# A window-attention and linear-attention kernel: layer 0's means subtracted on VectorE, its factors spread by kind, the last softmax inverse formed in SBUF, and another order

## The chip, the cores and the metric

The kernel runs on one core of one Trainium2 chip. The metric is the device time of one execution in microseconds (us). PE is TensorE, DVE is VectorE, ACT is ScalarE, POOL is GpSimd and SP is SyncE; ACT's and SP's queues also issue the DMAs of this kernel.

## The reference, cut to what matters

The input has 4 images of 128 channels and 64 x 64 pixels. Layer 0 norms over channels, adds a 3 x 3 depthwise convolution, and attends inside windows of 16 x 16 pixels, each query over its 5 x 5 neighbours. The patches are padded with zeros, so a neighbour outside the window counts with a logit of 0: it adds exp(0) = 1 to the denominator. Layer 1 is causal linear attention over the 4096 pixels of an image, then a recurrence over them with a batch norm in front.

```
# layer 0
y = _layernorm2d(x, ln_g, ln_b)                      # over channels
y = y + _cpe(y, cpe_w, cpe_b)                        # 3 x 3, depthwise
q, k, v = einsum(windows of y, Wq / Wk / Wv)         # 2 branches, 4 heads of 32
k_nb, v_nb = _patches(k, 5), _patches(v, 5)          # zero padded at the window's edge
attn = softmax(einsum(q, k_nb) * scale, axis=neighbours)
yb = (ho[:, 0] + LAM * ho[:, 1:].sum(axis=1)) / rect # ho: einsum(attn, v_nb), then Wo
x = x + yb
# layer 1
t = t + _L1_attn_ref(_ln_t(t), W, b)                 # elu + 1 features, causal sums
t = t + _L1_ffn_ref(_ln_t(t), W, V, gamma, beta)     # y_t = sigmoid(w_t + y_{t-1} V^T)
```

## The kernel before

**Tiling.** The work is cut into 16 bands (4 images, 4 bands of 16 rows each) and 64 windows, four a band; `places[i]` is the band and the column of window i. Layer 1 takes a band in two halves, called `a` and `c`; the halves of the band before it are `y` and `z` there. Where the order of the tail needs older ones, they are `v` and `w`.

**Layer 0's norm.** For bands 2 to 15 `norm_rows(n)` norms in two groups of tokens, of 4 columns of 128 tokens in the first and 3, 4 or 5 in the second. `measure_rows(g)` takes mean and variance on DVE from a copy of x with tokens on partitions, and POOL packs the means and forms the inverse deviations into `pk`. SP stores `pk` in DRAM (`sent`, a row of 2k numbers for each token), and `spread_rows(g)` on ACT's queue loads it back into every partition, as the tile `ahead`. There is one buffer for `ahead` and one for `rows`, so the spread and the load of the second group wait for the scaling of the first. `centre(g)` subtracts the means from `rows` on POOL (L413), `scale(g, ...)` multiplies by `ln_g` and the inverse deviation on DVE into the padded image `ypad` (L424). Both read the factors with a step of 2k elements. POOL then copies the edges of `ypad`, and the depthwise convolution runs as nine taps, the first on ACT (L498), the others on DVE (L500).

**Windows.** `window_inputs` makes q, k and v; `logits` the exponentials `es`; `weighted` has three steps. `sums` adds up the exponentials on PE and ACT copies them to `den` (L647), from which a DMA of SP collects one copy into `dc`. `values` forms the weighted values, which ACT copies to `o_sb` (L667). `inverse` adds the count of padded neighbours `pad_c` (L670) and takes the reciprocal (L672) on DVE, stores it in DRAM (`rd`, L676) and loads it spread over partitions (`rden`, L678); with every fourth window it checks the range of the sums (L633, L634). `scaled` multiplies `o_sb` by `rden` on POOL into the band's `oT` (L687).

**Layer 1.** `output0` projects `oT` on PE (L713) and adds x on DVE (L720). Then come `measure` and `norm` (POOL forms the inverse deviation, L314 and L315), `turn`, the features `queries` and `keys`, `values`, `scores`, `accumulate` (the running states, L822), `attend0` and `attend1` (L833 and L835 on PE; L843, L844 and L847 on DVE), `measure_last`, `send` (SP stores factors, L744), `spread` (ACT's queue loads them spread, L755), `keep` (L852) and `product` (L874, L875).

**Order.** PE, DVE, ACT and POOL run in the order in which the program is written: `in_order` ties each instruction to the one before it on its engine. SP is not tied. The order itself is in five tables. `START` has the first four windows. In the main loop each window goes through `SLOT`, in which names are steps of windows i-2 to i+1 and numbers are six gaps. In a gap the generator `layer1` advances by one entry of `LAYER1` (24 entries, over four windows, beginning with gap 0 of a band's second window), and then `front` by as many steps as `AHEAD[wj]` names that gap. `front` goes through `FRONT`: `n` is a step of the next band's norm, `d` and `c` pieces of the two halves of the convolution. `TAIL` has what is left after the last window's logits. After the first five entries of `FRONT`, which `START` does, the first number of `AHEAD` belongs to its sixth entry. `warm.k` puts k matmuls of zeros on PE ahead of the next bank that is taken (L288). All PSUM work of layers 0 and 1 goes through one ring of eight banks.

After layer 1 a fixed loop of 41 rounds runs the recurrence. The change doesn't touch it.

Of the kernel before, what the change touches and what calls it, by code (L numbers as in the profile page):

```python
# [45 lines left out]
    "measure_last.z product.y output.a send.z",  # L46
    "",
    "",
    "measure.a",
# [4 lines left out]
    "turn.a spread.z",  # L54
    "keep.z",
    "queries.a",
    "values.a keys.a product.z turn.c",
    "",
    "scores.a turn_keys.a keys.c queries.c accumulate.a",
    "attend0.a",  # L60
    "attend1.a turn_keys.c",
    "",
    "measure_last.a values.c",
    "",
    "keep.a",
    "",
    "send.a spread.a scores.c accumulate.c",
# [3 lines left out]
SLOT = ("sums", "values", "scaled", "logits", 0, "inverse", 1, "q", 2, 3, "k", "v", 4, 5)  # L71
AHEAD = ("013344", "023345", "022345", "01123")
START = (
    "upper conv.1 lower q.0 k.0 front mul.2 v.0",
    "logits.0 front front q.1 k.1 front v.1 conv.3",
    "logits.1 sums.0 mul.2 values.0 inverse.0 front q.2 warm.3",
    "front scaled.0 front front k.2 front front v.2",
    "front front logits.2 sums.1 front prepare values.1 inverse.1",
    "front load.2 front q.3 k.3 v.3 front front",
    "front sums.2 warm.2 front q.4 values.2 inverse.2 k.4",  # L80
    "front scaled.1 v.4 warm.1 front logits.3",
)
TAIL = (
    "output.y inverse.62 warm.1 output.z scaled.61 measure.z norm.z turn.z",
    "values.z warm.2 sums.63 measure.y norm.y turn.y queries.y keys.y",
    "warm.1 values.63 keep.w turn_keys.y send.w scores.y keys.z inverse.63",
    "warm.4 scaled.62 values.y accumulate.y turn_keys.z spread.w scaled.63 attend0.y",
    "queries.z attend1.y warm.1 measure_last.y send.y spread.y scores.z accumulate.z",
    "output.a product.w keep.y measure.a attend0.z warm.2 output.c attend1.z",
    "norm.a warm.2 measure_last.z product.v measure.c norm.c product.y keep.z",  # L90
    "turn.a keys.a values.a turn.c queries.a keys.c queries.c warm.2",
    "turn_keys.a scores.a accumulate.a send.z attend0.a attend1.a measure_last.a send.a",
    "turn_keys.c warm.2 values.c scores.c accumulate.c attend0.c attend1.c spread.z",
    "spread.a measure_last.c warm.2 warm.4 keep.a norm_last.c product.z turn_last.c",
    "keep.c product.a product.c",
)
FIRST = "nnnnnncccccccccc"
FRONT = "ndnnddndnddnncccccccccc"
# [19 lines left out]
def conv_attn_hybrid(ctx: ExitStack, tc: tile.TileContext, ins: dict, out: bass.AP):  # L118
# [50 lines left out]
    def groups(n):  # L169
        wi = bands[n][1]  # L170
        first, end = (0 if wi == 0 else 1), NCH + (wi < NB - 1)
        return first, first + 4, end
# [202 lines left out]
    def norm_rows(n):  # L375
# [8 lines left out]
        def measure_rows(g):  # L384
# [15 lines left out]
            sent[g] = dram4.tile([P, 2 * k], F32, tag=f"ahead{k}", name=f"ahead{k}")  # L400
            nc.sync.dma_start(sent[g], pk[:, : 2 * k])

        def spread_rows(g):
            k = sent[g].shape[1]
            f = p1.tile([P, P * 2 * 5], F32, tag="ahead", name="ahead")
            f = f[:, : P * k].rearrange("p (t k) -> p t k", k=k)
            nc.scalar.dma_start(f, sent[g].unsqueeze(0).to_broadcast([P, P, k]))
            fac[g] = f.rearrange("p t (m j) -> p m j t", m=2)

        def centre(g):  # L410
            j0, j1 = groups(n)[g : g + 2]
            v = rows[n, g][:, : (j1 - j0) * P].rearrange("p (j t) -> p j t", t=P)
            nc.gpsimd.tensor_tensor(v, v, fac[g][:, 0], ALU.subtract)  # L413

        def scale(g, dst, t0, t1):
            x, r = rows[n, g], fac[g][:, 1, t0 // P : -(-t1 // P), :]
            if t1 - t0 < P:
                src = x[:, t0:t1].rearrange("p (r w) -> p r w", w=W)
                r = r[:, 0, : t1 - t0].rearrange("p (r w) -> p r w", w=W)
            else:  # L420
                src = x[:, t0:t1].rearrange("p (j a w) -> p j a w", a=2, w=W)
                r = r.rearrange("p j (a w) -> p j a w", w=W)
                dst = dst.rearrange("p (j a) w -> p j a w", a=2)
            nc.vector.scalar_tensor_tensor(dst, src, ln_g, r, ALU.mult, ALU.mult)  # L424
# [213 lines left out]
    def weighted(w):  # L638
# [29 lines left out]
        yield  # L668

# [298 lines left out]
    def block(what):  # L968
# [10 lines left out]
        elif name == "logits":  # L979
            logits(windows[i])  # L980
        elif name == "scaled":
            if i not in scales:
                scales.add(i)
                scaled(*places[i], windows.pop(i))
        elif name in ("sums", "values", "inverse"):
            if name == "sums" and ("weighted", i) not in steps:
                steps["weighted", i] = weighted(windows[i]), ["sums", "values", "inverse"]
            run_of, left = steps["weighted", i]
            if name in left:
                assert left.pop(0) == name  # L990
                next(run_of)
# [51 lines left out]
    which.update(a=Half(len(bands) - 1, 0), c=Half(len(bands) - 1, 1))  # L1043
    v0 = bank()[:, :1]
# [861 lines left out]
```

## Time and profile before

| | us |
|---|---|
| runs | 842.4, 845.6, 853.11 (median 845.6) |
| profiled execution, its own time | 848.08 |
| its span, first to last instruction | 846.4 |
| DVE taps of the convolution (L500) | 187.6 busy, 240 instructions of 128x512 |
| POOL products with the inverse (L687) | 83.6 busy, 64 instructions |
| POOL subtractions of the means (L413) | 42.5 busy, 28 instructions |
| DVE scalings (L424) | 34.6 busy (with the instructions of the same tile, counted without overlap), 48 instructions |
| chain of waits, by engine | PE 44%, DVE 38%, DMA 7%, issue 4%, POOL 3%, ACT 3% |

The span has five stages: the start with the first windows (to about 54 us), bands of 46 us in the main loop, the tail after the last window's logits (from 735), and the recurrence (from 792). "Busy" counts the time in which an engine has an instruction of that group; an idle time is put down to what ended it. A busy PE is not a PE at its peak, since the ends of matmuls are modelled. The mean TensorE clock granted was 0.988 of full.

### The profile page before, as it was taken

How to read it: one execution, taken by the hardware profiler on the slowest of the kernel's cores; microseconds unless marked ns; L12 is line 12 of the kernel's file. 1: busy time of each engine (PE TensorE's matmuls, PEld its weight loads, DVE VectorE, ACT ScalarE, POOL GpSimd, SP SyncE). 2: the span in 40 equal slices, each digit the busy share in tenths (PEclk: the TensorE clock that was granted, in tenths of full speed). 3: DMA queues.
4: the chain of work that ended last, by engine and by line, in shares of the span. 5: the costliest groups of instructions: out<-in, count | busy, mean ns of one | idle time of the engine just before them, and what ended most of it. 6: DMA issues, size and time to landing. Idle time of an engine off the chain costs nothing.

```text
span 846.4 us, 28848 instructions
## 1 busy us (share of the span) xinstructions
PE 800.7 (95%) x11719; PEld 634.6 (75%) x11719; DVE 714.6 (84%) x2075; ACT 503.9 (60%) x983; POOL 309.6 (37%) x413
## 2 busy tenths in 40 slices
PE   9979999999999999999999999999999998988893
PEld 6658878778777778787777877787877777766793
DVE  7657898998998999999999989989898985477884
ACT  4746667465757475665647575656667574613683
POOL 3033444334343333444343434334443312222094
PEclk9998999999999999999999999999999999999997
DMA  5123342443443433434344334333342322211797
GB/s 155 38 81 106 98 126 72 125 118 94 126 104 105 119 106 88 139 81 140 87 108 119 89 110 131 104 97 122 86 147 68 96 66 49 71 56 44 236 221 182
DMA packets 93664, 91.27 MB, mean 108 GB/s; under 512 B 49745, under 2 KB 69329, under 8 KB 93521
## 3 DMA queue, kind: packets, MB, share of 16 engines
q1 hardware_dynamic: 62272, 51.96, 21.7%
q10 hardware_dynamic: 30240, 33.70, 13.8%
q0 software_dynamic: 1008, 3.67, 2.5%
q8 instruction: 94, 1.54, 0.8%
q14 instruction: 50, 0.40, 0.2%
HBM read 61.86 MB, written 18.00 MB: 94 GB/s over the span
## 4 chain that ended last, share of the span: by engine, by line
PE 44%; DVE 38%; DMA 7%; issue 4%; POOL 3%; ACT 3%; ACTq 0%; SPq 0%; POOLq 0%; DVEq 0%
DVE y L500 10%; PE bank L562 6%; PE z L1167 5%; PE bank L713 4%; DMA dc<-den 4%; PE bank L644 4%; PE bank L760 3%; DVE xn L322 3%; DVE ypad L424 3%; PE bank L615 3%; PE bank L575 3%; PE bank L659 2%; DVE st L310 2%; DVE x L847 2%; DVE state L822 2%
## 5 line engine op out<-in xcount | busy, mean ns | idle before, releaser
L500 DVE SCALAR_TENSOR_TENSOR y<-ypad,cpe_w,y 128x512 f32<-128x512 f32 x240 | 187.6, 782 | 7.3 <-ACT y L498 3.3
L687 POOL TENSOR_TENSOR oT<-o_sb,rden 128x512 f32<-128x512 f32 x64 | 83.6, 1306 | 232.9 <-DMA rden<-rd 123.0
L624 ACT ACTIVATE es<-bank 128x512 f32<-128x512 f32 x256 | 132.4, 608 | 20.1 <-PE bank L615 20.1
L659 PEld LDWEIGHTS bank<-es,v_sb 128*32 128x32 f32 x3072 | 63.0, 110 | 36.7 <-issue 35.3
L570 ACT COPY k<-bank 128x512 f32<-128x512 f32 x64 | 37.3, 583 | 84.4 <-DVE rd L844 24.4
L314 POOL TENSOR_SCALAR rs<-mv 128x4 f32<-128x4 f32 x68 | 27.2, 400 | 164.2 <-DVE mv L312 148.2
L615 PE MATMUL bank<-q,k 32*64 32x96 f32 (+1 forms) x4096 | 80.1, 277 | 5.3 <-ACT k L570 4.9
L713 PEld LDWEIGHTS bank<-woT,oT 128*128 128x128 f32 x512 | 63.6, 199 | 26.4 <-issue 17.8
L615 PEld LDWEIGHTS bank<-q,k 32*64 32x64 f32 x4096 | 74.5, 132 | 7.9 <-ACT k L570 5.2
L713 PE MATMUL bank<-woT,oT 128*128 128x128 f32 x512 | 66.3, 285 | 13.8 <-DVE x L847 8.7
L315 POOL TENSOR_TENSOR rs<-rs,mhalf 128x4 f32<-128x4 f32 x68 | 76.8, 1129 | 5.7
L644 PE MATMUL bank<-es,ones 128*32 128x512 f32 x512 | 69.8, 605 | 0.6 <-ACT es L624 0.6
L659 PE MATMUL bank<-es,v_sb 128*32 128x96 f32 (+1 forms) x3072 | 69.4, 237 | 0.0
L322 DVE TENSOR_SCALAR xn<-x,mv,rs 128x128 f32<-128x128 f32 x132 | 50.9, 447 | 21.1 <-POOL rs L315 21.1
L562 PE MATMUL bank<-y2w,wqT 128*128 128x256 f32 x256 | 67.9, 388 | 0.8 <-ACT y2w L532 0.5
L562 PE MATMUL bank<-y2w,wkT 128*128 128x256 f32 x256 | 65.9, 380 | 0.0
L575 PE MATMUL bank<-wvT,y2w 128*128 128x256 f32 x256 | 65.7, 379 | 0.0
L760 PE MATMUL bank<-xl,awT 128*128 128x512 f32 x128 | 63.2, 595 | 1.0 <-ACT xl L737 1.0
L310 DVE BATCH_NORM_STATS2 st<-x 128x6 f32<-128x128 f32 x256 | 55.3, 279 | 0.0
L570 ACT COPY q<-bank 128x512 f32<-128x512 f32 x64 | 38.1, 595 | 27.6 <-PE bank L562 21.5
L575 PEld LDWEIGHTS bank<-wvT,y2w 128*128 128x128 f32 x256 | 48.6, 190 | 6.6
L670 DVE TENSOR_TENSOR dc<-dc,pad_c 128x32 f32<-128x32 f32 x64 | 28.6, 447 | 28.2 <-DMA dc<-den 28.2
(159 smaller groups left out, 1732.0 us busy)
## 6 DMA issues: line engine op xcount, KB each, us to landing
rden<-rd SPq DMA_DIRECT2D x64, 256.0 KB
ahead<-ahead ACTq DMA_DIRECT2D x21, 512.0 KB
v_sb<-v_sb SPq DMA_DIRECT2D x128, 64.0 KB
factors<-factors ACTq DMA_DIRECT2D x31, 256.0 KB
xin<-in_xt SPq DMA_DIRECT2D x15, 512.0 KB
rows<-in_x SPq DMA_DIRECT2D x21, 256.0 KB
out<-rs_o ACTq DMA_DIRECT2D x16, 256.0 KB
resd<-rs_o ACTq DMA_DIRECT2D x16, 256.0 KB
```

The lines of the kernel that those rows point to most:

```text
L315: nc.gpsimd.tensor_tensor(rs[:, :n], rs[:, :n], mhalf[:, :n], ALU.pow)
L322: nc.vector.tensor_scalar(xn[:, j, :], piece, mv[:, j, 0:1], rs[:, j : j + 1], ALU.subtract, ALU.mult)
L500: nc.vector.scalar_tensor_tensor(y2, src, cpe_w[:, tap : tap + 1], y2, ALU.mult, ALU.add)
L562: nc.tensor.matmul(pps[:, br * WT : (br + 1) * WT], wT[:, br * P : (br + 1) * P], y2, start=True, stop=True,)
L575: nc.tensor.matmul(vps[:, e * 256 : (e + 1) * 256], y2[:, e * P : (e + 1) * P], wvT, start=True, stop=True,)
L615: nc.tensor.matmul(sps[h][half * KC : (half + 1) * KC, cols], w["k"][rows, k0 : k0 + KC], w["q"][rows, cols], start=False, stop=br == BR - ...
L624: nc.scalar.activation(es, sps[h], AF.Exp, scale=scale)
L644: nc.tensor.matmul(dps[rows], ones[:, :HD], w["es", h], start=True, stop=True)
L659: nc.tensor.matmul(ops[rows, cols], w["v"][:, n, c0 : c0 + HD], w["es", h][:, cols], start=(br, n) == pieces[0], stop=(br, n) == pieces[-1],)
L687: nc.gpsimd.tensor_tensor(oTs[n][:, :, :, wj * WS : (wj + 1) * WS], w["o"].rearrange("p (a r c) -> p a r c", a=BR, c=WS), w["rden"].rearra ...
L713: nc.tensor.matmul(yps[:, j * P : (j + 1) * P], oT[:, br, t], woT[:, br, :], start=br == 0, stop=br == BR - 1,)
L760: nc.tensor.matmul(zps, awT[:, m * P : (m + 1) * P], h.xl, start=True, stop=True)
```

## The change

Five things are changed.

- `centre` subtracts on DVE instead of POOL.
- The factors lie in DRAM as 2k rows of 128 tokens, first the k rows of means, then the k of inverse deviations. The store turns them (four bytes a piece), and the load spreads one contiguous row of 128 k x 2 numbers. `centre` and `scale` read contiguous factors, and `scale` needs one form for all sizes.
- The last window (63) has no `inverse` over DRAM. A tile `pad`, with the counts of padded neighbours for all queries, is loaded once by SP at the beginning of the tail into the buffer of `rows`. Then `inverse.63` handles the upper eight rows and `rest.63` the lower eight: each adds `den`, takes the reciprocal over 256 columns, and multiplies `o_sb` into `oT`, all on DVE. `check.63` does the last group's range check later. There is no `scaled.63` for this window.
- `LAYER1`, `SLOT`, `AHEAD`, `FRONT`, `START` and `TAIL` have another order.
- `TAIL` has four of the zero matmuls where it had 23; `START` has six in both.

```
@@ tables
 LAYER1 = (
-    "measure_last.z product.y output.a send.z",
+    "measure_last.z product.y output.a",
+    "send.z",
+    "measure.a",
     "",
-    "",
-    "measure.a",
     "output.c",
...
-    "turn.a spread.z",
-    "keep.z",
+    "turn.a spread.z keep.z",
+    "",
     "queries.a",
-    "values.a keys.a product.z turn.c",
+    "turn.c keys.a product.z",
+    "values.a",
+    "scores.a turn_keys.a keys.c queries.c accumulate.a values.c",
+    "attend0.a",
     "",
-    "scores.a turn_keys.a keys.c queries.c accumulate.a",
-    "attend0.a",
-    "attend1.a turn_keys.c",
+    "attend1.a measure_last.a",
+    "turn_keys.c send.a",
     "",
-    "measure_last.a values.c",
-    "",
-    "keep.a",
-    "",
-    "send.a spread.a scores.c accumulate.c",
+    "scores.c",
+    "keep.a spread.a",
+    "accumulate.c",
     "attend0.c",
     "attend1.c",
 )
-SLOT = ("sums", "values", "scaled", "logits", 0, "inverse", 1, "q", 2, 3, "k", "v", 4, 5)
-AHEAD = ("013344", "023345", "022345", "01123")
+SLOT = ("sums", "scaled", "values", "logits", 0, "inverse", 1, "q", 2, 3, "k", "v", 4, 5)
+AHEAD = ("023344", "012355", "012345", "01123")
...
-    "output.y inverse.62 warm.1 output.z scaled.61 measure.z norm.z turn.z",
-    "values.z warm.2 sums.63 measure.y norm.y turn.y queries.y keys.y",
-    "warm.1 values.63 keep.w turn_keys.y send.w scores.y keys.z inverse.63",
-    "warm.4 scaled.62 values.y accumulate.y turn_keys.z spread.w scaled.63 attend0.y",
...
+    "output.y output.z measure.y norm.y turn.y scaled.61 warm.4 keys.y",
+    "inverse.62 measure.z send.w norm.z sums.63 values.63 values.y scaled.62",
+    "inverse.63 turn_keys.y keep.w turn.z rest.63 queries.y keys.z scores.y",
+    "queries.z values.z product.v output.a measure.a spread.w product.w accumulate.y",
...
-FRONT = "ndnnddndnddnncccccccccc"
+FRONT = "nndndddnnddnncccccccccc"
@@ norm_rows
-            sent[g] = dram4.tile([P, 2 * k], F32, tag=f"ahead{k}", name=f"ahead{k}")
-            nc.sync.dma_start(sent[g], pk[:, : 2 * k])
+            sent[g] = dram4.tile([2 * k, P], F32, tag=f"ahead{k}", name=f"ahead{k}")
+            nc.sync.dma_start(sent[g].rearrange("k p -> p k"), pk[:, : 2 * k])
...
-            nc.scalar.dma_start(f, sent[g].unsqueeze(0).to_broadcast([P, P, k]))
-            fac[g] = f.rearrange("p t (m j) -> p m j t", m=2)
+            fac[g] = f[:, : P * k]
+            nc.scalar.dma_start(
+                fac[g], sent[g].rearrange("k p -> (k p)").unsqueeze(0).to_broadcast([P, P * k])
+            )
...
-            nc.gpsimd.tensor_tensor(v, v, fac[g][:, 0], ALU.subtract)
+            nc.vector.tensor_tensor(v, v, fac[g][:, :t], ALU.subtract)
@@ weighted, after o_sb is copied
+        if "pad" in w:
+            n, wj = places[w["at"]]
+            for half in range(2):
+                rs = slice(half * WS // 2, (half + 1) * WS // 2)
...
+                rden = view(w["pad"])
+                nc.vector.tensor_tensor(rden, view(den), rden, ALU.add)
+                nc.vector.reciprocal(rden, rden)
+                nc.vector.tensor_tensor(
+                    oTs[n][:, :, rs, wj * WS : (wj + 1) * WS], view(o_sb), rden, ALU.mult
+                )
+                yield
+            nc.vector.tensor_tensor(dc, dc, pad_c, ALU.add)
+            in_range(group)
+            yield
+            return
@@ before the tail
+    pad = p1.tile([P, 5 * P], F32, tag="rows", name="pad")[:, : BR * WT]
+    nc.sync.dma_start(pad, ins["pad_q"].partition_broadcast(P))
+    windows[len(places) - 1]["pad"] = pad
```

## The prediction

> **What bounds the kernel now.** I read the page's busy shares first, then the table of busy time by stage, one band of the main loop as a timeline, the groups by shape, and last the chain of work that ended last, through the tail.
>
> ```profile
> PE 800.7 (95%) x11719; PEld 634.6 (75%) x11719; DVE 714.6 (84%) x2075; ACT 503.9 (60%) x983; POOL 309.6 (37%) x413
> ```
> ```profile
> 238.00:284.00 46.00, 44.58 (x706) 35.53 (x705) 41.91 (x121) 28.19 (x52) 17.73 (x24) 1.00 0.42 108
> ...
> 744.00:790.00 46.00, 37.79 (x239) 27.86 (x238) 36.12 (x136) 12.16 (x20) 9.33 (x16) 1.00 0.20 57
> ```
> The columns are stretch, length, then busy us of PE, PEld, DVE, ACT, POOL. A band takes 46 us in the main loop: PE is busy 44 to 45.6 of them, DVE 41 to 43. In the tail both have room: PE 37.8, DVE 36.1. So the main loop holds about 1 us of PE idle a band; the tail holds more.
>
> The timeline of one band shows what that 1 us is:
> ```profile
> 284.66 1.14 DVE L633 TENSOR_SCALAR low_dc<-dc 128x128 bf16<-128x128 f32 x1
> 285.83 1.51 DVE L634 SCALAR_TENSOR_TENSOR low_dc<-dc,low_dc 128x128 bf16<-128x128 f32 x1
> ...
> 290.56 1.18 DVE L424 SCALAR_TENSOR_TENSOR ypad<-rows,ln_g,ahead 128x512 f32<-128x512 f32 x1
> ```
> ```profile
> 284.44 1.27 POOL L687 TENSOR_TENSOR oT<-o_sb,rden 128x512 f32<-128x512 f32 x1
> 285.68 1.51 POOL L413 TENSOR_TENSOR rows<-rows,ahead 128x512 f32<-128x512 f32 x1
> ```
> ```profile
> 295.20 0.61 DVE L847 SCALAR_TENSOR_TENSOR x<-bank,rd,x 128x128 f32<-128x128 f32 x2
> ...
> 295.95 0.79 PE L713 MATMUL bank<-woT,oT 128*128 128x128 f32 x5 [0.81 <-DVE x L847]
> ```
> PE's first product of the output projection (L713) stood 0.81 us because DVE was late with the attention's update (L847), which frees the PSUM bank. DVE was late because L634, which takes 0.29 us when alone, took 1.51: it ended at 287.3, just after POOL's centring (L413, 285.68 to 287.19). The list of waits has PE L713 waiting for DVE L847 10 times, 8.7 us.
>
> The chain through the tail:
> ```profile
> 744.14 2.08 DMA rd<-rc
> 746.35 3.85 DMA rden<-rd
> 750.34 1.27 POOL oT L687
> 751.66 2.05 PE bank L713 x16
> ```
> The last window's inverse goes to DRAM, comes back spread over partitions, and only then POOL scales and the last band's output can start. From there to the end of layer 1 (787.2) the chain alternates PE and DVE.
>
> **What the Trainium skill says.** "SBUF — State Buffer", section "Who interferes with whom": a VectorE instruction with two SBUF inputs, or one in a two-port mode, and a GpSimd instruction that reads SBUF lock each other out of a shared port for a whole instruction. The trace agrees: L634 291 ns at the shortest, 1374 at the median; L670 157 to 1384. L720, which reads PSUM and SBUF, kept its 0.67 us beside L413. "VectorE: DVE Perf Modes", section "The TRN2 errata": an fp32 tensor_tensor takes (N+151)/0.96 ns, 691 at 512 columns; the before has none of that shape from SBUF alone, but L1179 (256 columns) took 422 against 424 by that formula. "DMA: Bandwidth & Descriptors", "Rules for kernel authors": a strided last dimension becomes one descriptor per element; the stores of 1024 pieces in this trace are L856's. "TensorE: Matmul & The Clock Gate", Part 1: after an idle window of some 3.4 us the array runs at half rate. Here 2.75 us was enough: at 713.11 the 16 matmuls of L713 took 3.61 us against 1.78 to 2.05 elsewhere.
>
> **The change, part by part.** Layer 0's rows are normed so in bands 2 to 15, 28 groups.
>
> 1. *Centring leaves POOL.* L413's 42.5 us go. POOL is no bound (37%), but each took the shared port. Adding up, over the trace, what every DVE instruction took beyond its kind's short time gives 62 us; 40 of them end with POOL's L687, which stays, and 21.2 with L413. Gain on DVE: 21.2.
> 2. *Centring comes to DVE:* 21 x 0.691 + 3 x 0.824 + 4 x 0.557 = 19.2 us by the formula. Cost on DVE.
> 3. *The scaling reads its factors contiguously.* L424 now reads every eighth element: 1147 ns at 512 columns, 819 at 384, 448 at 128, 329 at 64. L500, the same operation with contiguous factors, has a median of 746 at 512 and 485 at 256: a slope of 1.02 ns a column over 224. So 17 x 0.40 + 11 x 0.20 + 10 x 0.09 + 10 x 0.04 = 10.3 us. Gain.
>
> Sum on DVE: 19.2 - 21.2 - 10.3 = -12.3 us, 0.9 us a band, about what PE stands. Bounds for what reaches PE: nothing (the PSUM bank is then freed by something else), and the whole idle time of PE from 64 to 698 us, 13 us. I take 8.
>
> 4. *The store of the factors* has 1024 four-byte pieces for 128 of 32 bytes. A four-byte packet takes 9 ns like a 32-byte one, 64 of them an engine, 0.6 us; L856's 1024 pieces left 1.3 to 2.3 us later than L401's 128. The spread on ACT's queue waits for it (319.59 store, 321.51 spread), and behind it stand ACT's copies; the copy that follows had 1.6 us of idle before it. So 0 to 0.7 us a band, no gain possible; I take 0, with 10 us kept for the range.
> 5. *Order of the main loop.* The same instructions. Centring 0 moves two steps later and stands right before its scaling; scaling 1 one step earlier (three DVE instructions, three POOL edges, one load on SP). The second-last attention's `send.a` leaves SP four steps earlier, `keep.a` and `spread.a` move by one. At 702.54 SP issued the factors' store ahead of the inverse's (702.95, ready at 701.57): 1.4 us, then the 6.20 us landing, 2.75 us of PE idle and a slow L713. Gain between -1 (another wait) and 4; I take 1.5. `scaled` and `values` swap, but one is on POOL alone and the other on none of POOL: nothing.
> 6. *START.* PE stands 4.88 us at 58.7, for ACT's copy L570, behind ACT's spread, which waits for L424's scaling of the first group. DVE before it lost 1.05 us to L413 and loses 0.4 less in L424, and gets 0.69: -0.8. The new order may do 2 us more or less. I take 1.
> 7. *The last inverse.* Gone: L670, L672, two DMAs, the product on POOL; from DVE 742.98 to 751.66, behind a DMA of `den`. New, twice over 256 columns: an add and a product (0.42 each, L1179) and a reciprocal. L672 takes 353 ns for 32 columns, L844 166 for two: 6.2 ns a column, 1.75 us at 256. One half 2.6 us. `den` was in SBUF at 738.85 and DVE stood idle 3.8 us just then; output could start at about 742, ten us earlier. The load of `pad` (256 KB) is issued with the tail's beginning and is hidden behind the windows that come first. Not all ten come: PE and DVE did other halves' work in that time. From 735.2 to 787.2 PE has 45.7 us of work, 8.1 of it 29 fills: 23 of the order and the six that end it. The new order has four for the 23, 5.3 us less: 40.4 remain. DVE's 36.7 become 40.8. The bound is thus 41 us for 52: a gain of at most 11, at least 0. I take 6.5.
>
> Sum: -8 - 1.5 - 1 - 6.5 = -17 us. The profiled execution took 848.1, so 831; it stands 2.5 over the median of 845.6, so **829** against that median.
>
> **The rivals.** A measurement of this kernel can tell about 2% (17 us) from no change.
>
> *DVE's relief is hidden.* For it: PE is busy 98% of a band and its spans hide waits; L687 stays and holds DVE longer in sum (40 us) than L413 did, and will run at other moments. Then only the tail counts: 845.6 - 6.5 = 839, 836 to 850 with the store's cost.
>
> *DVE waits for the factors (slower).* Centring 1 stood on POOL, idle anyway; on DVE everything queues behind it: the inverse's L670 and with it `rden`, the taps, both attentions' updates that free PE's banks. Its factors' last packets came 3.5 to 7 us after the issue. In most bands that is 2 to 3 us before DVE is done with `output.a` (L720); with 640 columns it is even with it, and POOL once waited 2.2 us. It decides where the landing comes more than 1 us after L720. At 2.2 us in each of 14 bands, 31 us, less the tail's 6.5: 870. Against it: the spread is issued at the same step as before, right after the scaling, which now ends earlier.
>
> *The tail goes cold.* Without 19 fills PE may stand over 2.7 us between dependent steps; each such place costs 1.6 us (3.61 against 2.0). Two or three eat most of the tail's gain: 834. This is inside the forecast's range.
>
> *It does not do what it says,* in that POOL's products then fall on other DVE work: counted under the first rival.
>
> **How the numbers follow.** Forecast case 0.54, own range 817 to 838; hidden 0.30; waiting 0.16, mostly past 862. The limit of faster by over 2% is 828.7, in the middle of the forecast's case: faster 0.46 (taking in a tail and loop that both come full), same 0.40, slower 0.14. Range 815 to 850.
>
> **What would show it.** Right: no L413 on POOL, a DVE subtraction near 0.69 us at 512 columns; L634's median near 0.3; L424 near 0.75; PE's wait for L847 before L713 gone; output of the last band some 8 us after its `den`; the tail from the last scores (735.2 in the old trace) to the recurrence some 45 us. Wrong: DVE idle before the subtraction, with the spread's landing as releaser; PE idle a band still at 1 us; gaps of over 2.7 us in the tail; a reciprocal well over 1.8 us.

## The result, and the profile after

| | us |
|---|---|
| after, median of 4 runs (1008.0 to 1013.0) | 1011.4 |
| before, median beside them | 844.0 |
| ratio, with its 95% interval | 1.195 [1.186, 1.205] |
| profiled execution after: span | 1011.1 |

The changed kernel is 167 us slower; the forecast was 829 us, and the range ended at 850. The busy shares of its page:

```profile
PE 858.3 (85%) x11700; PEld 673.9 (67%) x11700; DVE 687.8 (68%) x2108; ACT 493.6 (49%) x983; POOL 273.6 (27%) x384
```
DVE and POOL have less to do than before (714.6 and 309.6 us), as the change says. PE has all but 19 of its matmuls, is busy with them for longer, 858 us for 801, and yet has a smaller share. So nothing became a bound by its load: the engines wait. The groups by shape show the parts of the change that went as forecast:

```profile
L413 DVE TENSOR_TENSOR rows<-rows,ahead 128x512 f32<-128x512 f32 x21 | 14.4, 684 | 1.2 <-DMA ahead<-ahead 1.2
L417 DVE SCALAR_TENSOR_TENSOR ypad<-rows,ln_g,ahead 128x512 f32<-128x512 f32 x17 | 12.5, 736 | 0.5
...
L634 DVE SCALAR_TENSOR_TENSOR low_dc<-dc,low_dc 128x128 bf16<-128x128 f32 x16 | 4.7, 292 | 0.5
L680 DVE RECIPROCAL pad<-pad 128x256 f32<-128x256 f32 x2 | 3.5, 1753 | 0.1
```
After the bar stand busy us, mean ns of one, then idle time before them. The subtraction takes 684 ns, the scaling 736, the check's product 292 (it was 961 in the mean), the reciprocal 1753. And DVE hardly ever waits for the spread factors (1.2 us in all), which was the reason of the rival that forecast a slower kernel.

The list of waits (engine, line, what ended the wait; total us, times, longest) names the transfers:

```profile
POOL oT L707 <- DMA rden<-rd: 326.3, 34, 18.8
DVE dc L690 <- DMA dc<-den: 213.7, 22, 16.5
ACT k L570 <- DVE rd L864: 153.2, 13, 14.1
```
The same two waits in the before:

```profile
POOL oT L687 <- DMA rden<-rd: 123.0, 20, 9.1
DVE dc L670 <- DMA dc<-den: 28.2, 23, 5.7
```
The collection of `den` and the spread inverse, two DMAs that the change leaves as they were, are what DVE and POOL wait for. The third line of the list after misleads: the copy L570 was not held by DVE's `rd`. It stands on ACT's queue behind the spread of the factors. One band (58.5 us, before 46) on SP's queue, with start, duration, instruction:

```profile
212.00 0.38 SPq L400 DMA_DIRECT2D ahead<-pk  x1
212.43 0.57 SPq L696 DMA_DIRECT2D rd<-rc  x1
223.89 0.63 SPq L698 DMA_DIRECT2D rden<-rd  x1
...
225.12 0.38 SPq L400 DMA_DIRECT2D ahead<-pk  x1
...
227.20 0.64 SPq L652 DMA_DIRECT2D dc<-den  x1
```
and on ACT's:

```profile
223.79 0.33 ACTq L406 DMA_DIRECT2D ahead<-ahead  x1
224.16 0.58 ACT L570 COPY k<-bank 128x512 f32<-128x512 f32 x1 [8.61 <-PE bank L659]
```
The store of the factors (L400) is issued at 212.00. What needs it, ACT's spread (L406), leaves at 223.79. What doesn't need it, but was issued by SP just behind it, is late as well: `rd` left at 212.43, and `rden`, which waits for it, at 223.89. The chain of waits shows the same for the second store and the collection issued 2.1 us behind it:

```profile
212.00 11.71 DMA ahead<-pk
...
227.20 9.41 DMA dc<-den
236.63 0.20 DVE dc L690
```
In the before, a collection in this place took 1.94 us from issue to the instruction that uses it (the median of the 14 that follow a store). So each store of factors, 28 of them, holds itself and what SP issues behind it for some ten us, twice a band. PE then stands, and its granted clock falls. The page's row of that clock, with a digit for a fortieth of the span, after and before:

```profile
PEclk9979899898979889897998979799899979999997
```
```profile
PEclk9998999999999999999999999999999999999997
```
The mean is 0.915 for 0.988. In the trace these are 28 stretches with a granted clock of 0.5, 173 us together, each beside idle time of PE of 1.9 to 7.8 us; the before has 3 such stretches, 23 us. The matmuls of the logits (L615) take 0.42 us in the mean inside these stretches and 0.28 outside, which goes with PE's 57 further busy us.

### The profile page after: what moved, and what is told of

It is laid out like the page before. It is cut to its first block, busy times and chain, and to the rows that moved or that the text cites. A ratio compares the mean times of both kernels' runs of the same rounds, so it can differ in the third digit from the quotient of the medians.

```text
span 1011.1 us, 28794 instructions
## 1 busy us (share of the span) xinstructions
PE 858.3 (85%) x11700; PEld 673.9 (67%) x11700; DVE 687.8 (68%) x2108; ACT 493.6 (49%) x983; POOL 273.6 (27%) x384
## 4 chain that ended last, share of the span: by engine, by line
PE 40%; DMA 28%; DVE 14%; issue 6%; POOL 5%; ACT 4%; SPq 1%; ACTq 0%; POOLq 0%; DVEq 0%; another core or an unknown queue 0%
DMA dc<-den 11%; DMA ahead<-pk 10%; PE bank L644 4%; PE z L1191 4%; PE bank L733 4%; PE bank L615 4%; PE bank L562 4%; PE bank L659 3%; DMA rden<-rd 3%; PE bank L853 3%; PE bank L855 3%; PE bank L780 3%; DVE xn L321 2%; POOL rs L314 2%; PE bank L894 2%
## 5 line engine op out<-in xcount | busy, mean ns | idle before, releaser
L500 DVE SCALAR_TENSOR_TENSOR y<-ypad,cpe_w,y 128x512 f32<-128x512 f32 x240 | 180.4, 751 | 7.2 <-ACT y L498 2.8
L570 ACT COPY k<-bank 128x512 f32<-128x512 f32 x64 | 37.3, 583 | 270.4 <-DVE rd L864 153.2
L690 DVE TENSOR_TENSOR dc<-dc,pad_c 128x32 f32<-128x32 f32 x63 | 16.1, 256 | 213.8 <-DMA dc<-den 213.7
L853 PE MATMUL bank<-v,aT 128*128 128x129 f32 x256 | 63.4, 340 | 71.0 <-DVE aT L819 71.0
L853 PEld LDWEIGHTS bank<-v,aT 128*128 128x128 f32 x256 | 52.9, 247 | 77.3 <-issue 75.8
L615 PE MATMUL bank<-q,k 32*64 32x160 f32 (+1 forms) x4096 | 85.5, 292 | 4.3 <-ACT k L570 4.3
L314 POOL TENSOR_TENSOR rs<-rs,mhalf 128x4 f32<-128x4 f32 x68 | 83.8, 1233 | 5.7
L615 PEld LDWEIGHTS bank<-q,k 32*64 32x64 f32 x4096 | 80.7, 140 | 6.9 <-ACT k L570 4.6
L644 PE MATMUL bank<-es,ones 128*32 128x512 f32 x512 | 77.7, 664 | 6.8 <-ACT es L624 6.8
L562 PE MATMUL bank<-y2w,wqT 128*128 128x256 f32 x256 | 73.7, 414 | 0.0
L733 PEld LDWEIGHTS bank<-woT,oT 128*128 128x128 f32 x512 | 63.3, 196 | 12.3 <-POOL oT L707 5.9
L602 PE MATMUL bank<-mask_q,mask_k 32*64 32x512 bf16 x512 | 39.4, 404 | 36.0 <-ACT k L570 30.2
L733 PE MATMUL bank<-woT,oT 128*128 128x128 f32 x512 | 64.5, 280 | 3.5 <-POOL oT L707 3.5
```

Source lines behind the costliest of these rows:

```text
L314: nc.gpsimd.tensor_tensor(rs[:, :n], rs[:, :n], mhalf[:, :n], ALU.pow)
L500: nc.vector.scalar_tensor_tensor(y2, src, cpe_w[:, tap : tap + 1], y2, ALU.mult, ALU.add)
L562: nc.tensor.matmul(pps[:, br * WT : (br + 1) * WT], wT[:, br * P : (br + 1) * P], y2, start=True, stop=True,)
L615: nc.tensor.matmul(sps[h][half * KC : (half + 1) * KC, cols], w["k"][rows, k0 : k0 + KC], w["q"][rows, cols], start=False, stop=br == BR - ...
L644: nc.tensor.matmul(dps[rows], ones[:, :HD], w["es", h], start=True, stop=True)
L733: nc.tensor.matmul(yps[:, j * P : (j + 1) * P], oT[:, br, t], woT[:, br, :], start=br == 0, stop=br == BR - 1,)
```

## The experiments

**Which part.** Four kernels, each with one part undone or done alone. The reference is the kernel before, run beside them (845.1 us).

The changed kernel with its factors stored and read as before, in rows of tokens; all else is the change's:

```
-            sent[g] = dram4.tile([2 * k, P], F32, ...)
-            nc.sync.dma_start(sent[g].rearrange("k p -> p k"), pk[:, : 2 * k])
+            sent[g] = dram4.tile([P, 2 * k], F32, ...)
+            nc.sync.dma_start(sent[g], pk[:, : 2 * k])
```


> The changed kernel with one part undone: the factors go to DRAM as before, one row of 2k numbers for each token, and are read with a step of 2k; centring on DVE, the last inverse in SBUF and the new order stay. Theory 'the four-byte store': the store of 1024 four-byte pieces is what costs; in the changed kernel it is complete some 11 us after its issue, and holds ACT's queue (the spread) and all that SP stores behind it. Then this kernel takes 820 to 850 us, and the spread leaves about 2 us after the store. Rival 'the order': the new tables put the store, the spread and the inverses badly; then it stays over 950. Rival 'centring on DVE': DVE waits for the factors; then it stays over 900, with DVE idle in front of the subtraction.


Measured: 850.0 us, 1.007 [1.004, 1.010].

The kernel before with the turned store and contiguous factors alone; centring stays on POOL:

> The kernel before with that part alone: factors stored as rows of one kind (1024 four-byte pieces) and read contiguously; centring stays on POOL, order and last inverse as before. Theory 'the four-byte store': 980 to 1030 us, the spread about 11 us behind its store, and DVE waiting for dc<-den over 100 us in sum where it waited 28. Rivals 'the order' and 'centring on DVE': 840 to 855, since only a few hundred four-byte packets of 9 ns are added.


Measured: 1018.8 us, 1.203 [1.197, 1.209]. Its waits are those of the changed kernel:

```profile
POOL oT L688 <- DMA rden<-rd: 336.0, 36, 15.3
DVE dc L671 <- DMA dc<-den: 218.7, 25, 16.5
```

The kernel before with `centre` on VectorE alone (`nc.gpsimd.tensor_tensor` becomes `nc.vector.tensor_tensor`), its factors read with the old step:

> The kernel before with the subtraction on DVE alone (strided factors). By the prediction's sum: DVE gets 28 subtractions of strided factors, at some 1.15 us for 512 columns (as L424), 30 us, and is freed of 21 us of holds by POOL's subtraction: some 9 us more of DVE work, so 842 to 856 us. Rival 'centring on DVE' (DVE waits for the factors, everything behind it): 870 or more, with DVE idle over 1 us in front of most subtractions.


Measured: 850.7 us, 1.006 [1.004, 1.008].

The kernel before with the last inverse in SBUF alone, `rest.63` in the place of `scaled.63` in the old order:

> The kernel before with the last window's inverse formed in SBUF, in the old order (rest.63 where scaled.63 stood, check.63 before the last scores). Prediction's step: output of the last band can start several us earlier, of which the old order of PE leaves only a part: 838 to 845 us, and a reciprocal of 256 columns takes 1.75 us. Rival: the DVE work (5 us) displaces the other halves' work and nothing is gained: 845 to 850.


Measured: 849.7 us, 1.006 [1.003, 1.008].

The turned store, alone with its contiguous factors, gives the whole loss, and without it the loss is gone. Centring on DVE alone costs 5.6 us, the last inverse alone 4.6.

**What of the store costs.** If the pieces were done when their packet records end, 1.7 us after the issue, the store could not hold anything. A spare store that nothing reads, behind the old one in the kernel before, takes the store's reader out of the question; its pieces can then be laid out at will.

```
+            junk = dram4.tile([2 * k, P], F32, ...)          # adjacent: 4 bytes apart
+            nc.sync.dma_start(junk.rearrange("k p -> p k"), pk[:, : 2 * k])
```
```
+            junk = dram4.tile([2 * k, P, P], F32, ...)       # far: 512 bytes apart
+            nc.sync.dma_start(junk[:, :, 0].rearrange("k p -> p k"), pk[:, : 2 * k])
```


> The kernel before with one more store for each of the 28 groups: the same factors, turned, as 1024 four-byte pieces (1280 and 768 in some groups) into a DRAM buffer that nothing reads, issued by SP right behind the old store. Theory (each four-byte piece costs about 150 ns of its DMA engine's time until it is written, and SP's later transfers are not told done before it): nobody waits for the spare store itself, the spread of the factors still leaves about 2 us after the old store, but the collection of den and the inverse that SP issues next land about 8 to 10 us late; VectorE's wait for the collection of den rises from near nothing to 150 us or more in sum, and the time is 950 to 1020 us. Rival (the pieces are done when their packet records end, 1 us after the start, and only the spread that reads them was late): no wait of VectorE or GpSimd over 20 us more, time 845 to 855 us.

> The same spare store, but each four-byte piece lands 512 bytes from the next. Theory (a price for each piece, wherever it lands): the same waits and time as with adjacent pieces, within 10 us. Rival (pieces that share one line of DRAM wait for one another[...]): the pieces no longer meet in one line, the collection of den lands within 3 us of its issue, and the time is 845 to 865 us. If it is slower than with adjacent pieces, the pieces gain from lying together.


Measured: adjacent 1033.5 us, far 853.2 (one run each; the kernel before is at 846.5). The wait for the collection, first with adjacent pieces, then with far ones:

```profile
DVE dc L672 <- DMA dc<-den: 235.0, 23, 17.5
```
```profile
DVE dc L672 <- DMA dc<-den: 36.6, 26, 5.7
```
So nobody has to read what is stored: the store holds the DMAs behind it. And not only those of SP's queue. With adjacent pieces ACT's spread of a band's first group, issued 0.3 to 2.4 us behind the spare store, lands 10.4 us after its own issue (median of 13 bands, by its last signal in the trace; in the fourteenth it left 11.0 us behind the store and took 4.4); in the before it takes 4.0 us, with far pieces 4.4. It reads only the old store. But my theory of a price for each four-byte piece falls: as many pieces, and as small, cost little when they lie 512 bytes apart. What costs is that they lie together.

The changed kernel with pairs (a mean and its inverse deviation, 8 bytes): 512 pieces a store, adjacent; centring and scaling read with a step of two:

```
-            sent[g] = dram4.tile([2 * k, P], F32, ...)
+            sent[g] = dram4.tile([k, P, 2], F32, ...)
+            nc.sync.dma_start(sent[g].rearrange("k p m -> p k m"), both)
```


> The changed kernel with half as many pieces: 8 bytes (a mean and its inverse deviation), 512 for 1024; the load spreads 128 tokens of pairs and both readers step by two elements. Theory (price per piece, about 155 ns on each of 16 engines): 32 pieces an engine, so the spread leaves about 1 + 32 x 0.155 = 6 us after the store's issue instead of 10.8, the collection of den is held about 4 to 5 us instead of 9.5, and of the 167 us over the kernel before less than half is left: 890 to 930 us. Rival (price per byte or per store): the spread leaves 10 us after the issue or later and the time is over 980 us.


Measured: 850.4 us, 1.004 [1.002, 1.006]. The spread leaves 3.2 to 4.6 us after the store where it isn't held by its buffer (8.8 to 11.8 in the changed kernel, 1.4 to 2.8 before). Both are below what I expected. At the time it looked as if a hold of two or three us cost nothing; what it costs comes out below.

Two more spacings of the spare store's four-byte pieces, and a short one: 16 tokens only, whose pieces of one kind fill 64 bytes, the kinds 512 bytes apart.

```
+            junk = dram4.tile([2 * k, P, 2], F32, ...)       # half: 8 bytes apart
+            junk = dram4.tile([2 * k, P, 16], F32, ...)      # 64 bytes apart
+            nc.sync.dma_start(junk[:, :16].rearrange("k p -> p k"), pk[:16, : 2 * k])   # short
```


> The kernel before with the spare store again, its four-byte pieces 8 bytes apart (64 in 512 bytes of DRAM, where the adjacent ones have 128 and the far ones 1). As many pieces, on as many engines, as in both. Theory (what costs is how many pieces share one stretch of DRAM): half as dense is about half the hold, as with the 8-byte pairs: the collection of den that follows lands 5 to 7 us after the spare store instead of 11, and the time is 850 to 920 us. Rival (what costs is that the pieces of four bytes touch, so that nothing lies between them): no hold at all, 845 to 855 us. Rival (a piece of four bytes costs what it costs as soon as others are in its 512 bytes): as with the adjacent pieces, 1000 us or more.

> The spare store with its four-byte pieces 64 bytes apart (8 in 512 bytes). Theory (the hold grows with the pieces that share 512 bytes or less): 8 of 128, below 1 us of hold, nothing to be seen: 845 to 856 us. Rival (any sharing of 512 bytes is dear): VectorE's wait for the collection of den over 100 us, time over 900 us.

> The spare store cut to 16 tokens: for each kind 16 adjacent four-byte pieces, which fill 64 bytes, each kind 512 bytes from the next; 128 pieces in all (160 and 96 in some groups). Theory A (pieces that share 64 bytes wait for one another, some 0.6 to 0.7 us each): every 64 bytes has 16 pieces as in the full store, so the hold is the same: the collection of den lands about 10 us after its issue, time over 980 us. Theory B (pieces that share 512 bytes wait for one another, 0.09 us each): 16 pieces in 512 bytes, 1.4 us, over before the collection is issued: 2 us to land, 845 to 855 us.


The results together, with one from below; "landing" is the time from the issue of the collection of `den` to the DVE instruction that uses it, where that waited and a store stood less than 4 us ahead, as a median. "Completion" is the store's own: a DMA raises its semaphore by sixteen signals, and this is the time from its issue to the last of them, as a median of the stores that have all sixteen in the trace. The kernels with a spare store ran once each; the other times are medians.

| store | pieces in 512 bytes | completion, us | landing, us | store to landing, us | time, us |
|---|---|---|---|---|---|
| none but the old one (before) | 16 of 32 bytes | 1.8 | 1.94 | 4.8 | 846 |
| spare, short | 16 of 4 bytes | 2.2 | 1.95 | 4.4 | 849.5 |
| spare, far | 1 | 3.3 | 2.12 | 4.5 | 853.2 |
| spare, 64 bytes apart | 8 | 3.1 | 2.02 | 4.4 | 848.9 |
| spare, half | 64 | 4.9 | 3.45 | 6.5 | 876.5 |
| changed, pairs | 64 of 8 bytes | 4.5 | 4.26 | 6.6 | 850.4 |
| changed, quads (below) | 32 of 16 bytes | 2.6 | 2.16 | 4.9 | 857.2 |
| spare, adjacent | 128 | 11.3 | 10.01 | 12.1 | 1033.5 |
| changed | 128 | 10.9 | 9.52 | 11.6 | 1011.4 |

From 64 pieces in 512 bytes to 128 the landing moves from 6.5 to 12.1 us behind the store, some 0.09 us a piece; with 32 or fewer next to nothing is to be seen, because the collection itself ends later than the store. The completions show that this slope isn't one for all densities: a spare store of all the pieces takes 1.8 us more at 64 than at 8, and another 6.4 us at 128. Pieces of 4 and of 8 bytes with one density hold alike. That theory A (16 pieces in the same 64 bytes are enough) fell with the short store is clear. That the stretch is 512 bytes is not: the short store has an eighth of the pieces. The split store was to settle it, with all the pieces, in eight DMAs, 16 in each 512 bytes:

```
+            junk = dram4.tile([2 * k, 8, P], F32, ...)
+            for c in range(8):
+                nc.sync.dma_start(junk[:, c, :16].rearrange("k p -> p k"), pk[16 * c : 16 * c + 16, : 2 * k])
```


> All pieces of the adjacent spare store (1024 for four columns of tokens), but in eight DMAs of 16 tokens each, and the 64 bytes that 16 tokens of a kind fill lie 512 bytes from the next. Eight issues on SP take some 3 us. Theory A (64 bytes): 16 pieces share 64 bytes, the hold is that of the adjacent store, 10 us or more, time over 980 us. Theory B (512 bytes): 16 pieces share 512 bytes, 1.4 us for each DMA, next to no hold; time 850 to 880 us, from SP's seven further issues.


Measured: 1004.4 us, A's time, but a landing of 2.58 us, B's. What stands in its chain of waits is one of the spare stores itself, then SP:

```profile
285.95 5.57 DMA junk<-pk
291.59 0.50 SPq L589
```
SP waited for a spare store to finish before it issued the next transfers, so the collection was late in leaving rather than in landing. In this program the DMAs take eight semaphores in turn, and each waits for its semaphore's last use: eight spare stores take all eight, and L589 stood for that of the first. So the time says nothing for A. The completions do say something against B. The first of the eight stores, with as many pieces as the short one, is complete 5.3 us after its issue, where the short one took 2.2, and all eight 9.4 us after the first issue (medians); B put 1.4 us on each. Neither theory holds as it was stated. How the number of pieces, the length of the stretch and the packing inside it act together stays open.

**Another way to rows of kinds.** The changed kernel with the factors turned on DVE and stored as 128-byte pieces:

```
+            nc.vector.transpose(turned, pk)              # 32 x 32 blocks, at the beginning of the next step
+            for q in range(0, P, 32):
+                nc.sync.dma_start(sent[g][:, q : q + 32], turned[q : q + k, :])
```


> The changed kernel with the factors turned on VectorE (one 32x32-block transpose of 128x32 for each group, a step later) and stored as pieces of 128 bytes by four DMAs of SP; factors still lie in DRAM by kind and are read contiguously, centring is on VectorE, order and last inverse are those of the change. Theory (only the four-byte pieces cost; the other steps of the prediction hold): the spread leaves about 2 to 4 us after the stores' issue, VectorE's waits for the collection of den vanish, the scaling takes 0.75 us at 512 columns, and the time is the prediction's 829 us plus 28 transposes of about 0.25 us: 832 to 842 us. Rival (VectorE's relief does not reach TensorE, as the kernel with the old rows of tokens at 850 us hints): 843 to 855 us.


Measured: 911.0 us, 1.076 [1.073, 1.079], outside both. The stores were quick: the spread left 1.2 to 3.2 us after the last of them. But they, and with them SP's order, had moved a step:

```profile
247.34 1.28 SPq L408 DMA_DIRECT2D ahead<-pkT  x4
253.02 0.34 SPq L774 DMA_DIRECT2D factors<-rs  x1
...
254.70 0.64 SPq L662 DMA_DIRECT2D dc<-den  x1
```
SP was done with the stores at 248.6 and then stood at the attention's store (L774) until POOL had its `rs`, at 253.0. The collection of `den`, behind it, left at 254.70. In the changed kernel and in the one with pairs the same store (L764) comes after that collection. SP, which issues in order, turned the delay of one transfer into one of another: a band takes 52 us. In sum SP waits 116.5 us for `rs`, where it waits 68.4 in the before. That this is what costs the 65 us is read from the trace; no run puts the stores back in their place.

**The rest of the change.** The new tables alone; the new tail and the last inverse with the old main loop; and the new tables with the last inverse, centring and factors as before.

```
 (tables of LAYER1, SLOT, AHEAD, FRONT, START and TAIL of the change, scaled.63 where rest.63 stands)
 (TAIL of the change and the inverse in SBUF; the other tables as before)
 (all tables of the change and the inverse in SBUF)
```


> The kernel before with the new tables of order alone; the last inverse still goes over DRAM (its product stands where rest.63 stands), centring stays on GpSimd, the factors stay in rows of tokens. The prediction's steps 5 and 6 expect -2.5 us against the kernel before, and fewer zero matmuls in the tail may give some of what step 7 counted: 838 to 846 us. Rival (the new order is made for the new operations and without them something waits): 848 to 858 us, with the wait to be seen in the tail at the last product.

> The kernel before with the last inverse formed in SBUF and the new order of the tail alone; main loop, start, centring and factors are those of before. In the kernels tried so far with the new tail it took 41 to 42 us from the last window's sums to the last copy of an output, in those with the old one 44 to 47. Theory (of the change's steps the tail alone gains, some 4 us): 840 to 843 us, 0.3 to 0.7% less than before. Rival (the tail's gain needs the new main loop, which leaves it other work): 844 to 848 us.

> The changed kernel with the factors in rows of tokens and the means subtracted on GpSimd, both as before: the kernel before with the whole new order and the last inverse in SBUF. With centring on VectorE this was 850.0 us (1.0069). Theory (centring on VectorE with strided factors costs some 0.5%, as it did alone; order +0.3%, tail -0.4%): 844 to 848 us. Rival (the new order needs centring on VectorE, and the prediction's steps 5 and 6 would show only with it): 850 us or more.


Measured: order 849.4 us, 1.003 [1.001, 1.005]; tail with inverse 845.1, 0.998 [0.996, 1.000]; order with inverse **842.6, 0.996 [0.994, 0.998]**, the only one of the three whose interval lies below 1. The order without the inverse gains nothing, and the inverse in the old order loses (1.006 above): in the first PE stands 5.9 us in the tail for the product that still comes over DRAM, in the second the lower half's product is formed 10.4 us after `den`, at its late place in the old order. Each needs the other.

**The relief of VectorE, without the store.** The kernel with pairs had DVE 28 us freer in the main loop, and the loop was no shorter: either the relief doesn't reach PE, or the pairs' own hold takes it back. Two kernels tell this apart. Both store the factors in rows of tokens, as before, and read the wrong ones: contiguously, as the change does. They don't compute the reference's norm, but the transfers and the work are right.

```
-            nc.vector.tensor_tensor(v, v, fac[g][:, 0], ALU.subtract)
+            nc.vector.tensor_tensor(v, v, flat[g][:, : (j1 - j0) * P], ALU.subtract)
...
+                flat[g][:, t + t0 : t + t1].rearrange("p (r w) -> p r w", w=W),   # in scale
```


> The changed kernel with its factors stored and spread in rows of tokens, as before, but centring (on VectorE) and scaling read them contiguously, so that each token is normed with another token's numbers: layer 0's norm of bands 2 to 15 computes something else, the work and the transfers are the change's in all but the four-byte store. It has steps 1 to 3 and 5 to 7 of the prediction in full, and no store that holds SP. The prediction's sum for these is 829 us against a median of 845.6, a ratio of 0.980. Rival (DVE's relief is hidden, and of the change only order and last inverse gain): as the kernel with the new order, the last inverse and centring on GpSimd, 0.996, or within 0.3% of it.

> The kernel with the new order and the last inverse, centring on GpSimd with the old step, and only the scaling reading its factors contiguously (each token scaled with another token's numbers; layer 0's norm of bands 2 to 15 computes something else). Step 3 of the prediction alone: VectorE has some 12 us less to do. If VectorE's relief reaches TensorE it is 5 to 10 us faster than the same kernel with strided factors (842.6 us): a ratio of 0.985 to 0.990. If the relief is hidden: 0.994 to 0.998.


Measured: 824.4 us, **0.975 [0.971, 0.979]**, with both; 831.5 us, 0.986 [0.981, 0.991], with the scaling alone. The relief reaches PE. The main loop, from the copy of the first sums of band 2 to that of band 15 (stretch, length, then busy us of PE, PEld, DVE, ACT, POOL), before, with contiguous reads, and with pairs:

```profile
110.50:707.10 596.60, 583.45 (x9089) 465.43 (x9093) 543.59 (x1577) 370.31 (x677) 228.87 (x294) 1.00 0.38 105
```
```profile
107.60:687.00 579.40, 578.07 (x9093) 462.38 (x9095) 525.87 (x1602) 365.79 (x677) 196.04 (x269) 1.00 0.39 109
```
```profile
111.30:710.10 598.80, 585.89 (x9095) 463.80 (x9097) 515.78 (x1602) 364.86 (x678) 198.20 (x270) 1.00 0.39 105
```
With contiguous reads the loop is 17.2 us shorter. 12 of them are PE's idle time (13.2 us before, 1.3 left); the other 5 come out of PE's busy time for the same matmuls, at the same granted clock, so its spans had hidden waits. (DVE is busier here than with pairs, 525.87 for 515.78 us: L633 of the range check takes 717 ns in the mean, 167 with pairs.) The waits of PE in this stretch are nearly gone; first the before, then the kernel with contiguous reads:

```profile
PE bank L713 <- DVE x L847: 8.7, 10, 0.9
```
```profile
PE bank L733 <- POOL oT L707: 2.2, 2, 1.9
PE bank L733 <- DVE x L867: 0.6, 2, 0.3
```
So the pairs' hold of some two us a store cost 26 us (850.4 - 824.4; 24 by the ratios), about as much as the half-dense spare store did in the kernel before (876.5 - 846.4 = 30, one run). The profile with pairs is of a quick execution, 844.5 us, and its loop is still no shorter.

**Between the two.** If 16 bytes a piece and a step of four elements were both cheap, the gain could be had in full. Quads hold mean and inverse deviation of two columns:

```
+            nc.sync.dma_start(
+                sent[g][0, :n4].rearrange("(a p j) -> p a j", p=P, j=4),
+                both[:, : 2 * a].rearrange("p (a j) m -> p a (j m)", j=2),
+            )
```


> The changed kernel with pieces of 16 bytes (mean and inverse deviation of two columns of tokens; 32 pieces in 512 bytes of DRAM), contiguously spread; VectorE reads with a step of four elements and needs some 50 instructions more (7 us in all), and one or two stores a group. A last column without a partner is stored in pairs of 8 bytes. Theory (the hold grows with the pieces that share 512 bytes, and a step of four costs VectorE no more than one of two): the collection of den lands 2 to 2.5 us after its issue, where it took 4.3 with pairs, and most of the kernel with contiguous reads (824 us) comes back: 828 to 838 us, ratio 0.98 to 0.99. Rival (a step of four is read as slowly as one of eight, 1.09 us a subtraction at 512 columns): 840 to 850 us. Rival (a hold is left from 32 pieces as from 64): landing over 3 us, 845 us or more.


Measured: 857.2 us, 1.011 [1.007, 1.015]. The store no longer holds (landing 2.16 us), but the subtraction is as slow as with the old step of eight (1087 ns):

```profile
L423 DVE TENSOR_TENSOR rows<-rows,ahead 128x512 f32<-128x512 f32 x24 | 26.3, 1096 | 0.0
```
The first rival had the cause; the time is 7 us past its range, with the scalings in smaller pieces (45 of 256 columns at 667 ns) besides. In sum DVE is busy 730.6 us, where it is 699.7 with contiguous reads, about what the time differs by. Of the layouts tried, none has both a store that holds nothing and a step of one or two for DVE.

## Why the prediction was wrong

**Step 4 failed**, the store of the factors: "64 of them an engine, 0.6 us", "0 to 0.7 us a band", "I take 0, with 10 us kept for the range". It costs 187 us, which is the changed kernel less the one with contiguous reads and the old store (1011.4 - 824.4): 6.7 us for each of the 28 stores. The rest of the sum came close, 829 us for the 824.4 of the kernel without the four-byte store, but in part by luck: steps 1 to 3 gave some 18 us where I took 8, steps 5 to 7 3.6 where I took 9, and the two errors offset each other.

The step had the number of pieces right and took two things for prices that aren't. A packet's record is not its completion: in the changed kernel the 1024 pieces of a band's first group also start between 0.9 and 1.7 us after the issue, with 7 ns each in the mean, and the spread that waits for them leaves some 11 us after it. And the store I held it against, L856's, has as many pieces, but of 256 bytes (256 KB in 1024): it says nothing of pieces of four bytes that lie together. The Trainium skill, "DMA: Bandwidth & Descriptors", "Specifications", has the warning that I passed over: below 512 bytes a DMA engine reads and writes back. That would explain why pieces that share a stretch wait for one another, but no run shows the reading; what the runs show is that lying together costs, and smallness alone little (3.3 us to completion with the pieces far apart, 11.3 with them adjacent).

The step also looked for who waits for the store and found ACT's spread. It didn't ask what is issued behind it. The same page, "Queues, rings and completion order", says that a DMA's signal lands only after every earlier write of the same engine. The trace agrees: the collection lands 9.5 us after its issue for 1.9. That put the inverse of the windows near a store on the path, and DVE, POOL and PE behind it.

The other steps:

- *Steps 1 to 3, DVE's load:* 8 us taken, of 12.3 less on DVE; they brought more. The prices were right: centring takes 684 ns at 512 columns (formula 691), 19.0 us in all (19.2); the scalings' sum falls from 36.3 to 24.5 us (forecast 10.3 less). From the kernel with order and inverse (0.996) the scaling takes the time to 0.986, which is 8 to 9 us; centring on DVE with contiguous factors takes it to 0.975, 9 more, where steps 1 and 2 sum to 2 (each of the two to some 5 us, by the intervals). The main loop alone gained 17.2 us where I had put a bound of 13, PE's idle time: a busy PE held waits too. The rival "DVE's relief is hidden" falls. With factors still read in the old step centring takes 1087 ns, and on DVE costs 5.6 us when done alone.
- *Step 5, the loop's order:* 1.5 us taken. The three profiles that have the new order, DVE's old reads and no spare store show 599 to 604 us for the loop, four with the old order 597 to 600. No gain to be seen.
- *Step 6, the start:* 1 us taken; the copy of the first sums of band 1 comes at 60.4 to 61.7 us in five profiles with the new order and the old store, at 64.5 in the before and at 63.5 to 64.4 in six others with the old order and no hold. Some 2 to 4.
- *Step 7, the last inverse:* the reciprocal took 1.753 us for 1.75. The last band's output starts 5.7 to 6.8 us after `den` is copied, with the new tail order (forecast some 8; before 12.8). From that copy of `den` to the last copy of an output (`rs_o`, on ACT) the tail takes 40.1 to 41.3 us, for 45.1 in the before and 43.7 to 44.4 in eight others with the old tail and inverse: 2 to 5 us, where I took 6.5. PE had no gap above 1.8 us there in these kernels, so the fills that went were not missed, and "the tail goes cold" falls.

Of the rivals, the slower one had the right side and the wrong transfer: DVE did wait, but for the collection of `den`, not for the factors. Steps 5 to 7 together give -3.6 us (-5.3 to -1.8) for -9; steps 1 to 3 some -18 for -8.

## What to carry to other kernels

Before a store is turned in DRAM, count how many pieces lie together in one short stretch of it, not only how many there are, and price it by the instruction that waits for its completion, or by its last signal, in a trace with the same layout; packet records don't show it. Then list what is issued in the ten us behind it, on the other queue too, because here all of that completed later. To learn what a change would bring without its one bad step, let a kernel read the wrong data in the right shape: here it showed that all of the rest was worth 2.5%.

## What the runs showed that I had not expected

- 1024 four-byte pieces take 11 us to completion when 128 share 512 bytes, 4.9 at 64, and 3.1 to 3.3 at 8 or 1 in 512 bytes. Their packet records look alike: 7 ns each in the mean, begun by 1.6 us after the issue, both for far and for adjacent pieces (a band's first group).
- The hold reaches DMAs of the other queue: ACT's spread takes 10.4 us to land behind the adjacent spare store, 4.0 without it.
- Reading every second float from SBUF cost DVE what contiguous reading did (684 and 737 ns at 512 columns with pairs; 684 and 736 in the changed kernel). Every fourth cost as much as every eighth (1096 against 1087 ns for the subtraction).
